# Two self-attention stages of a four-layer network: values projected inside the query/key loop, score banks claimed first, four banks for the projections

## The chip, the core and the metric

The kernel runs on one core of a Trainium2 chip, in one launch. The metric is the device time of one execution in microseconds. A profile is one further execution, recorded by the hardware. Engines are named as in the profile: PE is TensorE's matmul (PEld its weight load), DVE VectorE, ACT ScalarE, POOL GpSimd, SP the engine that issues most transfers.

## The reference, cut to what matters

Twelve stages run in a row on `x` (16 sequences of 64 tokens, width 256, float32): four layers of cross attention, self attention and feed-forward. Each reads a layer norm of `x` and adds its output to `x`, so no stage can begin before the one before it has finished the rows that it needs. Two of the twelve are touched:

```python
# layer 0 self attention (16 heads of 16), causal softmax
cq = gelu(x @ wq + bq);   ckv = gelu(x @ wkv + bkv)          # 256 -> 64
q = gelu(concat(cq @ wqc + bqc, rope(x @ wqr + bqr)))
k = gelu(concat(ckv @ wkc + bkc, rope(x @ wkr + bkr)))
v = ckv @ wv + bv
out = softmax(mask(q k^T / 4)) v @ wo + bo
# layer 1 self attention (16 heads of 16), causal linear attention
q, k, v = split(x @ w_qkv.T + b_qkv);   q, k = elu(q) + 1, elu(k) + 1
out = (cumsum(k v) q) / (cumsum(k) q + 1e-6) @ w_out.T + b_out
```

## The kernel before, in words

The 1024 tokens lie as 8 tiles of 128 rows, two sequences to a tile. Both stages have the same two parts.

**Projections.** `norm_T` (L347) turns the normalised rows into `xnT` (features on partitions, 1024 tokens along the row) with sixteen PE transposes and four copies. Then queries and keys are projected in halves of 512 tokens, one PSUM bank each.

- `L0_attn` (L1037) has four jobs `(d, h)`: d is 0 for queries and 1 for keys, h the half. `narrow` projects to 64 columns and ACT applies Gelu into `cl[d]`. `turned` projects the rotary part; ACT copies its two halves swapped into `sw`, and DVE makes `r`, `sw` and their sum (L1087, L1091). `wide`, one job later, projects `cl[d]` up to 128 columns, and `gelu` takes it and `r` through ACT: for queries straight into `qT`, for keys into `g`, from which DVE writes two masked copies into `k2` (L1102).
- `L1_attn` (L1233) has eight blocks: for each half h, c = 0, 1 (queries) and c = 2, 3 (keys). ACT makes `e` and `z` (L1262, L1263), DVE joins them (L1265), and for keys also writes two masked copies into `k2` (L1267).

After the last of these, `pair_values` (L1008) makes the values. POOL clears `V` and writes its two columns of ones (L1014, L1016; no order is imposed on these). Four times it then takes a bank, has PE project two token tiles into it, and has DVE add the bias in four instructions of 64 partitions (L1030).

**Attention.** A software pipeline over the 8 tiles. `scores(t)` writes 128 queries by 64 keys for all heads into half of `S4`, a tile of four banks; DVE masks it (L1142 `Sx` in layer 0, L1293 `A` in layer 1). In layer 0 a row maximum (L1149, DVE), its subtraction (L1150, POOL), an exponential (L1153, ACT) and transposes (`turn`) follow. `values(t)` multiplies by `V` and DVE divides (`pair_attend`, L1192), `back(t)` transposes, `out(t)` projects and `finish_x` adds to `x` and takes the next layer norm's statistics.

**What sets the order.** Between `self.fixed = True` and `False`, `mm`, `tr` and everything in `pinned` (L193) keep program order on their engine, so PE, ACT and DVE of these stages run as written. The allocator hands out PSUM banks; a matmul into a reused bank waits for the last reader of what was in it. The projections' pool `pst` has 6 banks (L1053, L1249). It is closed before the pool of `S4` is opened (L1123, L1275), so `S4` lies on banks that the projections and the values have used, and the first scores wait for the last bias addition of `V`.

Of the kernel before, what the change touches and what calls it, by code (L numbers as in the profile page):

```python
# [12 lines left out]
ALU = mybir.AluOpType  # L13
AX = mybir.AxisListType
PSUM = bass.MemoryType.PSUM

P = 128
B, S, D = 16, 64, 256
NT = B * S // P
# [157 lines left out]
class Net:  # L177
# [827 lines left out]
            "L0_attn_wv", "L0_attn_wo",  # L1005
        )

    def pair_values(self, pool, pp, xT, w, bias):  # L1008


        nc = self.nc
        n, k = w.shape[1], xT.shape[0]
        V = pool.tile([P, NT, 2, 8, 34], F32, tag="V", name="V")
        nc.gpsimd.memset(V, 0.0)  # L1014
        for i in range(2):
            nc.gpsimd.memset(V[i * S : (i + 1) * S, :, :, :, 32 + i], 1.0)  # L1016
        bias = bias.rearrange("p (a i f) -> p a i f", i=2, f=16)
        for t in range(0, NT, 2):
            ps = self.psum(pp, [P, 2, 8, 2, 16], "pst")
            for u in range(2):  # L1020
                for kc in range(n):
                    self.mm(
                        ps[:, u].rearrange("p a i f -> p (a i f)"),
                        xT[:, kc, (t + u) * P : (t + u + 1) * P], w[:k, kc, :],
                        kc == 0, kc == n - 1,
                    )
            for b in range(2):
                r = slice(b * S, (b + 1) * S)
                for i in range(2):
                    self.pinned(nc.vector.tensor_tensor(  # L1030
                        V[i * S : (i + 1) * S, t : t + 2, b, :, i * 16 : (i + 1) * 16],
                        ps[r, :, :, i, :], bias[r, :, i, :].unsqueeze(1).to_broadcast([S, 2, 8, 16]),
                        ALU.add,
                    ))
        return V

    def L0_attn(self, w):  # L1037


        nc, tc = self.nc, self.tc  # L1040
        wq, wkv, wqc, wkc, wqr, wkr, wv, wo = w
        with (
            tc.tile_pool(name="l0a", bufs=1) as wk,
            tc.tile_pool(name="l0am", bufs=4) as small,
        ):
            qT = wk.tile([P, 2, NTOK], F32, tag="qT", name="qT")

            k2 = wk.tile([P, 2, 2, NTOK], F32, tag="k2", name="k2")
            self.fixed = True
            with (  # L1050
                tc.tile_pool(name="l0an", bufs=1) as wn,
                tc.tile_pool(name="l0as", bufs=2) as sp,
                tc.tile_pool(name="l0a_t", bufs=6, space=PSUM) as pst,  # L1053
            ):
                xnT = self.norm_T(wn, pst, "pst")
                self.add_bias(1)
                jobs = [(d, h) for d in range(2) for h in range(2)]
                cl = [wn.tile([64, 1, NTOK], F32, tag=f"cl{d}", name="cl") for d in range(2)]
                names = (
                    (wq, "bq", wqc, "bqc", wqr, "bqr"), (wkv, "bkv", wkc, "bkc", wkr, "bkr"),  # L1060
                )
                par = self.c("par")
                rot = {}

                def narrow(d, h):
                    w1, b1 = names[d][:2]
                    tok = slice(h * 512, (h + 1) * 512)
                    ps = self.psum(pst, [P, 512], "pst")
                    self.project_T(ps[:64, :], w1, xnT, slice(None), tok)
                    self.pinned(nc.scalar.activation(  # L1070
                        cl[d][:, 0, tok], ps[:64, :], AF.Gelu, bias=self.pv(f"L0_attn_{b1}")[:64, :]
                    ))

                def turned(d, h):

                    wr, br = names[d][4:]
                    tok = slice(h * 512, (h + 1) * 512)
                    ps = self.psum(pst, [P, 8, S], "pst")
                    self.project_T(
                        ps.rearrange("p b s -> p (b s)"), wr, xnT, slice(None), tok  # L1080
                    )
                    sw = sp.tile([P, 8, S], F32, tag="sw", name="sw")
                    self.pinned(nc.scalar.copy(sw[0:64], ps[64:128]))
                    self.pinned(nc.scalar.copy(sw[64:128], ps[0:64]))
                    r = sp.tile([P, 8, S], F32, tag="r", name="r")
                    for o, i, b, c in ((r, ps, br, "cos0"), (sw, sw, br + "~", "sin0")):
                        self.pinned(nc.vector.scalar_tensor_tensor(  # L1087
                            o, i, self.pv(f"L0_attn_{b}"),
                            self.c(c).unsqueeze(1).to_broadcast([P, 8, S]), ALU.add, ALU.mult,
                        ))  # L1090
                    self.pinned(nc.vector.tensor_tensor(r, r, sw, ALU.add))  # L1091
                    rot[d, h] = r.rearrange("p b s -> p (b s)")

                def gelu(d, h, c, src, bias=0.0):
                    tok = slice(h * 512, (h + 1) * 512)
                    if d == 0:
                        self.pinned(nc.scalar.activation(qT[:, c, tok], src, AF.Gelu, bias=bias))
                        return
                    g = sp.tile([P, 512], F32, tag="g", name="g")
                    self.pinned(nc.scalar.activation(g, src, AF.Gelu, bias=bias))  # L1100
                    for i in range(2):
                        self.pinned(nc.vector.tensor_scalar(  # L1102
                            k2[:, c, i, tok], g, par[:, i : i + 1], None, ALU.mult
                        ))

                def wide(d, h):
                    w2, b2 = names[d][2:4]
                    tok = slice(h * 512, (h + 1) * 512)
                    ps = self.psum(pst, [P, 512], "pst")
                    self.mm(ps, w2[:64, 0, :], cl[d][:, 0, tok])  # L1110
                    gelu(d, h, 0, ps, self.pv(f"L0_attn_{b2}"))
                    gelu(d, h, 1, rot[d, h])

                for n in range(len(jobs) + 1):
                    if n < len(jobs):
                        narrow(*jobs[n])
                        turned(*jobs[n])
                    if n:
                        wide(*jobs[n - 1])
                V = self.pair_values(wk, pst, cl[1], wv, self.bv(0))  # L1120
            with (
                tc.tile_pool(name="l0at", bufs=2) as sp,
                tc.tile_pool(name="l0a_s", bufs=1, space=PSUM) as pss,  # L1123
                tc.tile_pool(name="l0a_p", bufs=2, space=PSUM) as pst,
                tc.tile_pool(name="l0a_a", bufs=1, space=PSUM) as psa,
            ):
                S4 = self.psum(pss, [P, 4, 2, 2, 2, S], "S4")
                state = {}

                def scores(t):  # L1130
                    ps = S4[:, :, t % 2]
                    for kc in range(2):
# [33 lines left out]
                def values(t):  # L1166
                    acc = self.psum(psa, [P, 8, 34], "acc")
                    state[t] = self.pair_attend(sp, acc, V, state[t], t, 0.0)

# [63 lines left out]
    def L1_attn(self, w):  # L1233
# [3 lines left out]
        nc, tc = self.nc, self.tc  # L1237
        wqkv, wout = w
        bqkv = self.pv("L1_attn_b_qkv")
        with tc.tile_pool(name="l1a", bufs=1) as wk:  # L1240
            qT = wk.tile([P, 2, NTOK], F32, tag="qT", name="qT")

            k2 = wk.tile([P, 2, B, 2, S], F32, tag="k2", name="k2")
# [1 line left out]
            with (  # L1245
                tc.tile_pool(name="l1an", bufs=1) as wn,
                tc.tile_pool(name="l1am", bufs=4) as small,
                tc.tile_pool(name="l1as", bufs=3) as sp,
                tc.tile_pool(name="l1a_t", bufs=6, space=PSUM) as pst,  # L1249
            ):  # L1250
                xnT = self.norm_T(wn, pst, "pst")
                self.add_bias(4)
                for h in range(2):
                    tok = slice(h * 512, (h + 1) * 512)
                    for c in range(4):
                        ps = self.psum(pst, [P, 512], "pst")
                        self.project_T(ps, wqkv, xnT, slice(c * P, (c + 1) * P), tok)

# [2 lines left out]
                        bias = bqkv[:, c : c + 1]  # L1261
# [4 lines left out]
                        for i in range(2 * (c // 2)):  # L1266
# [2 lines left out]
                                z.rearrange("p (b s) -> p b s", s=S),  # L1269
                                self.c("par")[:, i : i + 1], None, ALU.mult,  # L1270
                            ))
                V = self.pair_values(wk, pst, xnT, wqkv[:, :, 512:768], self.bv(3))
            with (
                tc.tile_pool(name="l1at", bufs=2) as sp,
                tc.tile_pool(name="l1a_s", bufs=1, space=PSUM) as pss,  # L1275
                tc.tile_pool(name="l1a_a", bufs=2, space=PSUM) as psa,
            ):
                S4 = self.psum(pss, [P, 4, 2, 2, 2, S], "S4")
                state = {}

                def scores(t):
                    ps = S4[:, :, t % 2]
                    for kc in range(2):
# [1079 lines left out]
```

## Time and profile before

| what | us |
|---|---|
| three runs | 3265.1, 3266.31, 3282.47 (median 3266.31) |
| the profiled execution | 3275.31 |
| its span, first to last instruction | 3273.5 |
| PE busy in the span | 3021.5 (92%) |
| DVE, ACT, POOL busy | 1261.0, 1362.1, 371.6 |
| mean granted TensorE clock | 0.953 |
| layer 0: first projection to last matmul of the values | 520.79 to 544.48 |
| layer 0: first scores, first mask `Sx` | 552.88, 554.13 |
| layer 1: first projection to last matmul of the values | 1707.16 to 1729.66 |
| layer 1: first scores, first mask `A` | 1732.72, 1733.90 |

All times inside the trace count from the span's start. In a row of the timeline the columns are: start, duration of the whole group, engine, source line, operation, output and inputs with sizes, number of instructions, and in brackets the idle time before it on its engine and what ended it. A float32 matmul of the program is two PE instructions in the trace. A busy PE is not PE at full clock: the clock that was granted is a column of its own. The share of busy time is an average over twelve stages; for a change inside two of them, what counts is the row that waits last there.

### The profile page before, as it was taken

To read this page: it belongs to the slowest core of one execution; us is meant where nothing else is said; L and a number is where in the kernel's file an instruction comes from. 1 tells how busy PE (TensorE), PEld (TensorE's weight loads), DVE (VectorE), ACT (ScalarE), POOL (GpSimd) and SP (SyncE) were. 2 spreads that over 40 slices of the span, in tenths; PEclk is the share of its full clock that TensorE was granted. 3 is DMA by queue.
4 is the path that set the end of the run, shared out by engine and by line. 5 is a ranking of instruction groups with operands and counts; after the bars stand their busy time and mean duration, and the time that the engine had idled before them with its cause. 6 is when DMAs were issued, how large, how long until landed. Compare 5 with 4: busy or idle time off the path is not lost. (4 is left out here: it accounts for less than half of the span.)

```text
span 3273.5 us, 67440 instructions
## 1 busy us (share of the span) xinstructions
PE 3021.5 (92%) x28567; PEld 2263.0 (69%) x28567; DVE 1261.0 (39%) x3415; ACT 1362.1 (42%) x2699; POOL 371.6 (11%) x538
## 2 busy tenths in 40 slices
PE   7999997699799999999998999999979798889798
PEld 5666664599556666666666777777748676778697
DVE  6888884422244444444446521221242100035200
ACT  5888884211233333333333522222222387763111
POOL 0000001233200000000010000000012311111232
PEclk9999998699899999999997999999988899999799
DMA  6334431389211121211257011111208555510497
GB/s 216 106 130 134 134 108 42 134 287 323 63 61 61 61 81 44 78 61 61 81 174 221 28 46 55 61 41 61 77 17 300 161 180 187 175 56 1 152 328 241
DMA packets 178362, 395.09 MB, mean 121 GB/s; under 512 B 11446, under 2 KB 142270, under 8 KB 165214
## 3 DMA queue, kind: packets, MB, share of 16 engines
q1 hardware_dynamic: 165070, 372.91, 33.0%
q0 software_dynamic: 11712, 16.00, 2.4%
q8 instruction: 225, 3.69, 0.5%
q10 hardware_dynamic: 1280, 1.88, 0.2%
q14 instruction: 75, 0.61, 0.1%
HBM read 375.02 MB, written 16.12 MB: 119 GB/s over the span
## 5 line engine op out<-in xcount | busy, mean ns | idle before, releaser
L199 PE MATMUL acc<-ctx,st 128*128 128x257 f32 (+1 forms) x1664 | 397.2, 383 | 0.0
L199 PE MATMUL pss<-qk,ctxT 128*128 128x512 f32 (+1 forms) x832 | 388.8, 592 | 0.6 <-DVE qk L634 0.6
L199 PEld LDWEIGHTS acc<-ctx,st 128*128 128x128 f32 (+1 forms) x1664 | 310.1, 190 | 94.6 <-issue 35.6
L459 DVE CUSTOM_DVE_ANT_0 Sx<-s,mneg 128x384 f32<-128x384 f32 (+1 forms) x512 | 264.2, 570 | 88.6 <-PE s L199 88.6
L650 DVE TENSOR_TENSOR top<-pss,top 128x512 f32<-128x512 f32 x192 | 132.7, 691 | 402.4 <-ACT st L645 402.3
L203 PE MATMUL pst<-cst,Sx 128*128 128x128 f32 (+1 forms) x1736 | 255.8, 286 | 25.5 <-ACT Sx L1369 10.3
L674 ACT ACTIVATE st<-st 128x512 f32<-128x512 f32 (+1 forms) x208 | 130.6, 629 | 292.5 <-DVE st L673 292.5
L935 ACT ACTIVATE Pr<-pss 128x512 f32<-128x512 f32 (+1 forms) x512 | 219.9, 523 | 62.1 <-PE pss L199 60.7
L503 ACT ACTIVATE PT<-pst 128x384 f32<-128x384 f32 x512 | 215.1, 489 | 63.4 <-PE pst L203 62.3
L203 PEld LDWEIGHTS pst<-cst,Sx 128*128 128x128 f32 (+1 forms) x1736 | 188.7, 143 | 73.1 <-ACT PT L503 27.8
L199 PEld LDWEIGHTS pss<-qk,ctxT 128*128 128x128 f32 (+1 forms) x832 | 154.1, 186 | 120.7 <-issue 102.7
L645 ACT COPY st<-pss 128x512 f32<-128x512 f32 (+1 forms) x208 | 121.8, 585 | 201.5 <-PE pss L199 201.5
L199 PE MATMUL pso<-W,hT 128*128 128x256 f32 x884 | 200.9, 379 | 0.0
L199 PE MATMUL pst<-wst,ctxT 128*128 128x256 f32 (+1 forms) x832 | 183.4, 380 | 0.0
L199 PE MATMUL psk<-ctxT,wst 128*128 128x512 f32 (+1 forms) x512 | 181.8, 513 | 0.8 <-ACT qT L797 0.8
L199 PEld LDWEIGHTS pso<-W,hT 128*128 128x128 f32 x884 | 163.2, 190 | 19.7
L199 PEld LDWEIGHTS pst<-wst,ctxT 128*128 128x128 f32 (+1 forms) x832 | 153.5, 186 | 25.9 <-issue 2.7
L199 PE MATMUL pss<-q,ctxT 32*128 32x128 f32 (+1 forms) x3328 | 149.6, 298 | 13.6 <-issue 9.5
L199 PEld LDWEIGHTS psk<-ctxT,wst 128*128 128x128 f32 x512 | 88.3, 190 | 93.7 <-issue 92.1
L356 POOL TENSOR_TENSOR x<-x,bvec 128x256 f32<-128x256 f32 x40 | 29.8, 746 | 1079.2 <-ACT xn L317 1079.2
L837 DVE TENSOR_TENSOR v<-pst,bvec 128x512 f32<-128x512 f32 (+1 forms) x112 | 73.1, 653 | 204.4 <-PE pst L199 204.4
L478 ACT ACTIVATE Sx<-Sx,neg 128x384 f32<-128x384 f32 (+1 forms) x256 | 145.8, 620 | 11.5 <-DVE neg L469 11.3
(394 smaller groups left out, 4479.5 us busy)
## 6 DMA issues: line engine op xcount, KB each, us to landing
ctxT<-in_ctxT_dram SPq DMA_DIRECT2D x64, 1601.0 KB
W<-in_L_experts_dram SPq DMA_DIRECT2D x61, 1024.0 KB
ctx<-in_ctx_dram SPq DMA_DIRECT2D x32, 1536.0 KB
W<-in_L_experts_dram SPq DMA_DIRECT2D x23, 1536.0 KB
ctx<-in_ctx_ones_dram SPq DMA_DIRECT2D x16, 1632.0 KB
ctx<-in_ctx_one_dram SPq DMA_DIRECT2D x16, 1542.0 KB
W<-in_L_experts_dram SPq DMA_DIRECT2D x23, 768.0 KB
W<-in_L_experts_dram SPq DMA_DIRECT2D x15, 1028.0 KB
```

The lines of the kernel that those rows point to most:

```text
L199: self.pinned(self.nc.tensor.matmul(out, lhsT, rhs, start=start, stop=stop))
L203: self.pinned(self.nc.tensor.transpose(out, in_, self.ident[:n, :n]))
L356: self.nc.gpsimd.tensor_tensor(self.x[:, t, :], self.x[:, t, :], self.bv(i), ALU.add)
L459: self.pinned(nc.vector.tensor_tensor_reduce(out=Sx[:, j, :n], in0=ps[j][:, :n], in1=st["mneg"][:, o : o + n], op0=ALU.add, op1=ALU.max, s ...
L478: self.pinned(nc.scalar.activation(Sj[j], Sj[j], AF.Identity, bias=st["neg"][:, j - 2 : j - 1]))
L503: self.pinned(nc.scalar.activation(PT, ps, AF.Exp))
L645: pin(nc.scalar.copy(st[:kn], ps[:kn]))
L650: pin(nc.vector.tensor_tensor(top[b][:kn], ps[:kn], top[b][:kn], ALU.max))
L674: pin(nc.scalar.activation(st, st, AF.Exp, scale=HD**-0.5))
L837: nc.vector.tensor_tensor(o, ps[:kn, :n, :], bv[:kn].to_broadcast([kn, n, D]), ALU.add)
L935: nc.scalar.activation(st["Pr"][:kn, g : g + n, j, :], ps[j][:kn, :n, :], AF.Silu)
```

## The change

`pair_values` is split. What is left of the name allocates `V` and has POOL clear it; the new `two_values(V, t, ...)` does one quarter of the rest: four (layer 0: two) matmuls into one bank, and four additions.

```diff
+    def two_values(self, V, t, pp, xT, w, bias):
...
+        ps = self.psum(pp, [P, 2, 8, 2, 16], "pst")
+        for u in range(2):
+            for kc in range(n):
+                self.mm(
...
+        for b in range(2):
...
+            for i in range(2):
+                self.pinned(self.nc.vector.tensor_tensor(
```

In layer 0 the keys' jobs come first, and two quarters of the values follow `wide` of each of the keys' two jobs. `S4` is opened at the top of the stage, with a pool of its own, and `pst` has 4 banks:

```diff
+            tc.tile_pool(name="l0a_s", bufs=1, space=PSUM) as pss,
         ):
+            S4 = self.psum(pss, [P, 4, 2, 2, 2, S], "S4")
...
-                tc.tile_pool(name="l0a_t", bufs=6, space=PSUM) as pst,
+                tc.tile_pool(name="l0a_t", bufs=4, space=PSUM) as pst,
...
-                jobs = [(d, h) for d in range(2) for h in range(2)]
+                jobs = [(d, h) for d in (1, 0) for h in range(2)]
...
+                V = self.pair_values(wk)
                 for n in range(len(jobs) + 1):
                     if n < len(jobs):
                         narrow(*jobs[n])
                         turned(*jobs[n])
                     if n:
                         wide(*jobs[n - 1])
-                V = self.pair_values(wk, pst, cl[1], wv, self.bv(0))
+                    if 1 <= n <= 2:
+                        for t in (4 * n - 4, 4 * n - 2):
+                            self.two_values(V, t, pst, cl[1], wv, self.bv(0))
```

In layer 1 `S4` and `pst` change in the same way, and a quarter of the values stands ahead of blocks 0 and 2 of each half:

```diff
+                V = self.pair_values(wk)
                 for h in range(2):
                     tok = slice(h * 512, (h + 1) * 512)
                     for c in range(4):
+                        if c % 2 == 0:
+                            self.two_values(
+                                V, 4 * h + c, pst, xnT, wqkv[:, :, 512:768], self.bv(3)
+                            )
                         ps = self.psum(pst, [P, 512], "pst")
...
-                V = self.pair_values(wk, pst, xnT, wqkv[:, :, 512:768], self.bv(3))
```

In the built program the number of instructions on each engine is the same, except for a few that only wait. The order of POOL's and SP's instructions does not change anywhere, and outside these two stages every instruction of every engine keeps its place and its waits.

More of the change, by code (lines that the diff above doesn't have):

```diff
@@ L1006, in load_L0_attn, with pair_values @@
         )
-    def pair_values(self, pool, pp, xT, w, bias):
+    def pair_values(self, pool):
         nc = self.nc
-        n, k = w.shape[1], xT.shape[0]
         V = pool.tile([P, NT, 2, 8, 34], F32, tag="V", name="V")
@@ L1016, in pair_values @@
             nc.gpsimd.memset(V[i * S : (i + 1) * S, :, :, :, 32 + i], 1.0)
+        return V
+    def two_values(self, V, t, pp, xT, w, bias):
+        n, k = w.shape[1], xT.shape[0]
         bias = bias.rearrange("p (a i f) -> p a i f", i=2, f=16)
[L1018 to L1035, printed above, removed]
+        ps = self.psum(pp, [P, 2, 8, 2, 16], "pst")
+        for u in range(2):
+            for kc in range(n):
+                self.mm(
+                    ps[:, u].rearrange("p a i f -> p (a i f)"),
+                    xT[:, kc, (t + u) * P : (t + u + 1) * P], w[:k, kc, :],
+                    kc == 0, kc == n - 1,
+                )
+        for b in range(2):
+            r = slice(b * S, (b + 1) * S)
+            for i in range(2):
+                self.pinned(self.nc.vector.tensor_tensor(
+                    V[i * S : (i + 1) * S, t : t + 2, b, :, i * 16 : (i + 1) * 16],
+                    ps[r, :, :, i, :], bias[r, :, i, :].unsqueeze(1).to_broadcast([S, 2, 8, 16]),
+                    ALU.add,
+                ))
     def L0_attn(self, w):
@@ L1119, in L0_attn @@
                         wide(*jobs[n - 1])
-                V = self.pair_values(wk, pst, cl[1], wv, self.bv(0))
+                    if 1 <= n <= 2:
+                        for t in (4 * n - 4, 4 * n - 2):
+                            self.two_values(V, t, pst, cl[1], wv, self.bv(0))
             with (
                 tc.tile_pool(name="l0at", bufs=2) as sp,
-                tc.tile_pool(name="l0a_s", bufs=1, space=PSUM) as pss,
                 tc.tile_pool(name="l0a_p", bufs=2, space=PSUM) as pst,
@@ L1126, in L0_attn @@
             ):
-                S4 = self.psum(pss, [P, 4, 2, 2, 2, S], "S4")
                 state = {}
@@ L1239, in L1_attn @@
         bqkv = self.pv("L1_attn_b_qkv")
-        with tc.tile_pool(name="l1a", bufs=1) as wk:
+        with (
+            tc.tile_pool(name="l1a", bufs=1) as wk,
+            tc.tile_pool(name="l1a_s", bufs=1, space=PSUM) as pss,
+        ):
+            S4 = self.psum(pss, [P, 4, 2, 2, 2, S], "S4")
             qT = wk.tile([P, 2, NTOK], F32, tag="qT", name="qT")
@@ L1248, in L1_attn @@
                 tc.tile_pool(name="l1as", bufs=3) as sp,
-                tc.tile_pool(name="l1a_t", bufs=6, space=PSUM) as pst,
+                tc.tile_pool(name="l1a_t", bufs=4, space=PSUM) as pst,
             ):
@@ L1255, in L1_attn @@
                     for c in range(4):
+                        if c % 2 == 0:
+                            self.two_values(
+                                V, 4 * h + c, pst, xnT, wqkv[:, :, 512:768], self.bv(3)
+                            )
                         ps = self.psum(pst, [P, 512], "pst")
@@ L1271, in L1_attn @@
                             ))
-                V = self.pair_values(wk, pst, xnT, wqkv[:, :, 512:768], self.bv(3))
             with (
                 tc.tile_pool(name="l1at", bufs=2) as sp,
-                tc.tile_pool(name="l1a_s", bufs=1, space=PSUM) as pss,
                 tc.tile_pool(name="l1a_a", bufs=2, space=PSUM) as psa,
             ):
-                S4 = self.psum(pss, [P, 4, 2, 2, 2, S], "S4")
                 state = {}
```

## The prediction

> **What bounds the kernel now.** I read the page first. PE is busy 92% of the span, so only stages in which PE stands still can give much; the chain that ended last is scattered over a dozen lines and names neither stage. So I asked the view of waits for the two stretches that the change touches (waiting engine and line, releaser, total us, times, longest).
>
> ```profile
> DVE r L1087 <- ACT sw L1084: 12.4, 4, 5.3
> ...
> PE S L199 <- DVE V L1030: 8.4, 1, 8.4
> ```
>
> ```profile
> PE S L199 <- DVE V L1030: 3.1, 1, 3.1
> DVE wa L1760 <- DMA wst<-in_L_w2T_dram: 2.2, 1, 2.2
> ```
>
> In both stages the first scores wait for the last bias addition of the values, 8.4 and 3.1 us. All of that is not yet a gain: the scores also need keys, queries and then DVE. So I read the timeline of layer 0 there.
>
> ```profile
> 530.71 0.75 DVE L1087 SCALAR_TENSOR_TENSOR r<-pst,pvec,cst 128x512 f32<-128x512 f32 x1 [1.64 <-ACT sw L1084]
> ...
> 532.15 0.69 DVE L1091 TENSOR_TENSOR r<-r,sw 128x512 f32<-128x512 f32 x1
> ...
> 540.87 3.61 PE L199 MATMUL pst<-wst,cl 64*128 64x256 f32 x16
> ...
> 542.48 3.39 DVE L1102 TENSOR_SCALAR k<-g,cst 128x512 f32<-128x512 f32 x8
> ...
> 545.78 6.96 DVE L1030 TENSOR_TENSOR V<-pst,bvec 64x256 f32<-64x256 f32 x16
> ...
> 552.88 1.16 PE L199 MATMUL S<-k,qT 32*64 32x128 f32 x32 [8.39 <-DVE V L1030]
> 554.13 1.23 DVE L1142 TENSOR_TENSOR Sx<-S,cst 128x1024 f32<-128x1024 f32 x1 [1.40 <-PE S L199]
> ```
>
> PE has the values' matmuls done at 544.48, while DVE is behind: after the last rotary sum it has eight masked copies (3.39) and sixteen additions (6.96) left, in a row. DVE is the late engine. Ahead of that it had gaps: each rotary group waits for ACT's `sw` copies, 12.4 us in four waits. Layer 1:
>
> ```profile
> 1707.16 15.60 PE L199 MATMUL pst<-xnT,wst 128*128 128x512 f32 x32
> ...
> 1722.59 7.07 PE L199 MATMUL pst<-wst,xnT 128*128 128x256 f32 x32
> ...
> 1722.79 0.69 ACT L1262 ACTIVATE e<-pst,pvec 128x512 f32<-128x512 f32 x1 [0.45 <-PE pst L199]
> ...
> 1724.82 0.88 DVE L1267 TENSOR_SCALAR k<-z,cst 128x512 f32<-128x512 f32 x2
> 1725.62 6.96 DVE L1030 TENSOR_TENSOR V<-pst,bvec 64x256 f32<-64x256 f32 x16
> ...
> 1732.72 1.12 PE L199 MATMUL S<-qT,k 32*128 32x64 f32 x32 [3.06 <-DVE V L1030]
> 1733.90 1.23 DVE L1293 TENSOR_TENSOR A<-S,cst 128x1024 f32<-128x1024 f32 x1 [1.32 <-PE S L199]
> ```
>
> Here PE works to 1729.66 without a gap, and DVE's additions end 3 us later.
>
> Last, the table by stretches (stretch, its length, busy us of PE, PEld, DVE, ACT and POOL, granted clock, DMA share, GB/s):
>
> ```profile
> 531.00:545.00 14.00, 13.49 (x38) 5.98 (x36) 8.41 (x16) 8.44 (x15) 0.00 (x0) 1.00 0.01 2
> 545.00:553.00 8.00, 0.12 (x8) 0.15 (x16) 7.53 (x19) 1.17 (x1) 0.00 (x0) 0.62 0.00 0
> 553.00:570.00 17.00, 11.12 (x208) 8.66 (x208) 10.46 (x10) 6.25 (x8) 7.61 (x4) 0.50 0.01 1
> 1711.00:1730.00 19.00, 18.66 (x60) 11.02 (x58) 14.20 (x28) 9.72 (x16) 0.00 (x0) 1.00 1.09 335
> 1730.00:1735.00 5.00, 1.12 (x32) 1.01 (x32) 3.61 (x7) 0.00 (x0) 0.00 (x0) 0.97 1.06 333
> 1735.00:1747.00 12.00, 11.82 (x166) 10.66 (x167) 5.50 (x10) 0.37 (x1) 0.00 (x0) 0.50 1.10 340
> ```
>
> Projections run at clock 1.00; after the first gap layer 0's pipeline runs at 0.50, and layer 1's soon after its own.
>
> **The change, layer 0.** No arithmetic is added: eight matmuls and sixteen additions of values move forward, and the keys' jobs change places with the queries'. The order of the built program gives DVE's list from the second rotary group on: rotary group, four copies into `k2`, two quarters of values; the same again; the last rotary group; then the first mask. Durations from the rows: a rotary group 530.71 to 532.84, 2.13 us; four copies 3.39/2 = 1.70; two quarters 6.96/2 = 3.48. From 530.71, where the second group starts in both kernels: 532.84, 534.54, 538.02 (values), 540.15, 541.85, 545.33 (values), 547.46. That is 16.75 us without a gap, if its inputs come in time. For that I walk PE: a `narrow`/`turned` pair takes 3.84 (row at 530.45), a `wide` 1.0, a quarter 0.90 (3.61/4). `wide` 0 ends at 530.4, two quarters at 532.2, the third pair at 536.0, `wide` 1 at 537.0, two quarters by 538.9, the fourth pair by 542.8, `wide` 2 at 543.8 and `wide` 3 at 544.7. ACT's copies for the third rotary group are then done by 537.4, DVE wants them at 538.0; for the fourth by 544.1, wanted at 545.3. So DVE is never kept waiting.
>
> The new wait: the first mask in the built program waits for ACT's last Gelu, of the fourth rotary group (0.62 and two hand-offs of about 0.05): 547.46 + 0.7 = 548.2. Behind it on DVE stands the whole attention pipeline. The scores themselves wait only for ACT's Gelu of the first half of queries, near 545.5, and take 1.25, ready by 546.8. So the first mask moves from 554.13 to 548.2, **5.9 us**. The 8.4 us wait is not the gain, because DVE still has its additions to make and is late again; what is won is its waiting for `sw` and nothing else.
>
> **Layer 1.** The order on DVE is a quarter of values, joins of two query blocks, a quarter, joins and four copies of two key blocks, and again. PE's sum is as before, so it ends near 1729.7; but its last matmuls are now those of a key block, not of values. Behind a key block's matmuls come two ACT steps, a join and two copies: in the old trace the last block's matmuls end at 1722.6 and its copies at 1725.7, 3.1 us. So DVE is free at 1732.8 and the first `A` begins there instead of at 1733.90: **1.1 us**. The 3.1 us wait of PE is exchanged for a tail of the same length on ACT and DVE. DVE's wait for the weights at 1709.78 plus the 2.29 reduction behind it now stands ahead of the first quarter's additions: done at 1713.8. The first key block takes their bank, and PE comes to it only at about 1715.8, so 2 us cover that; a load later by more than 2 us would be paid in full.
>
> **Four banks.** Reusing a bank earlier adds waits on PE, in front of everything queued there. Layer 0: the third quarter waits for the first one's additions (536.3, wanted 537.0), the fourth for ACT's Gelu of `wide` 1 (about 538.0, wanted 537.9), the fourth pair for the second quarter (538.0, wanted 538.9), `wide` 3 for the third quarter (543.6, wanted 543.8). Cost 0.1 to 0.3, hidden by DVE's list, which ends later. Layer 1: each block finds its bank free by 1.5 us or more. The first transposes of layer 1 now wait for the previous stage's last addition to `x`, ending at 1701.33, 0.8 us later than they started; the rest of them wait until 1706.5 for the last normalised rows anyway, so it costs nothing; without that cover, 0.8. POOL's clearing of `V` (3.73) keeps its place in POOL's queue in both stages, ahead of the statistics of the last tile; SP's queue is unchanged. The program behind the stages is unchanged too, and each stage starts from `x`, so a shift carries to the end. The next stage's weights are fetched only after routing, and from 519 to 615 the DMA share is 0.03 or less, so no transfer sets an end there that stays while the start moves.
>
> **Sum.** 5.9 + 1.1 = 7.0. Against the profiled execution: 3275.31 - 7.0 = 3268.3. That execution lies 9.0 above the median of the three runs; carried to the median, 3266.31 - 7.0 = **3259**.
>
> **A rule that speaks against it.** The Trainium skill, "TensorE: Matmul & The Clock Gate", section "A second HAM failure mode: psum-queue depth-cycling", tells of a kernel that cycled through its PSUM banks so that TensorE stood idle briefly between groups, and its clock swung between half and full. Fewer banks are a step that way. The row: with six banks the stretch 531 to 545 has PE busy 13.49 of 14.00 at clock 1.00. By my walk four banks add 0.3 us of gaps, so I stay with the row, 3259. By the rule the projections would drop to 0.50: layer 0's 14.3 us of matmul work from 530.4 on ends at 559.0 and the first mask, 2.1 us of rotary group and 0.7 later, comes near 561, +7; layer 1's 18.7 us from 1711 on end at 1748.4 and with the tail of 3.1 at 1751.5, +17.6. Together 3291.
>
> **Rivals.** *The clock holds in the pipelines* (0.14). The gap of PE ahead of layer 0's second scores shrinks from 8.4 to about 3 us, and layer 1's start changes. If the pipelines then ran at full clock: four transposes take 1.11 or 0.66 in the two clocks, so five tiles save 2.3; a turn of layer 1 has scores 1.99 or 1.12, values 1.93 or 1.13, projection 2.08 with transposes or 1.13 + 0.38, so four turns save up to 8. 3249. Against it: 553 to 570 has PE busy 11.1 of 17 and stays at 0.50, and the gaps between scores remain.
>
> *Nothing is won* (0.11): DVE's sixteen additions, now made while PE writes other banks, take longer. The gain of layer 0 is gone if the list of 16.75 takes 22.6, a third more. For it: nothing in the trace shows this mix. Against it: the first additions at 545.78 and the last have nearly one duration, 409 to 430 ns. 3266. That the change doesn't reach its aim (scores still waiting for the values) is excluded by the built order: their waits name ACT alone in layer 0 and nothing new in layer 1.
>
> *Slower* (0.09): the clock falls in the projections, as reckoned above, 3291. Half clock for t us costs t/2, so it decides from about 14 us at 0.50 in the two projections together.
>
> **Numbers.** The likeliest case, 0.66, has its own range 3253 to 3264 (the first masks within 1 us, the pipelines within 2 of their old length each). The three runs before scatter by 17 us, and a difference under 0.5% (16 us) is about what a measurement of this kernel can't tell from none. Faster by more: most of the clock's case and some scatter, 0.12. Slower by more: 0.09. Within: 0.79. The range, 3247 to 3270, takes in the clock's case in its upper part and the case of no gain; it leaves out the slower one.
>
> **What would show it.** Layer 0: the first mask near 548.2 (counted from an equal start), DVE without a gap from 530.7 to 547.5, PE's wait for `V` gone. Layer 1: PE without a gap to 1729.7, the first `A` near 1732.8 with the last copy of `k2` before it. Clock 1.00 in both projections. I am wrong if a projection shows 0.50, if PE waits for DVE by more than 1 us inside one, or if the pipelines of eight tiles change in length.

## The result, and the profile after

| | before | after |
|---|---|---|
| first series, median | 3277.48 us (3265.1 to 3287.73, 20 runs) | 3266.31 us (3258.15 to 3279.37, 20 runs) |
| ratio, 95% interval | | 0.9970 [0.9960, 0.9980] |
| second series, median | 3276.39 us (30 runs) | 3269.95 us (22 runs) |
| ratio, 95% interval | | 0.9982 [0.9972, 0.9993] |
| profiled execution, its span | 3275.31, 3273.5 us | 3270.24, 3268.5 us |
| mean granted clock in the span | 0.953 | 0.952 |

The change makes the kernel faster by 0.2 to 0.3%, which lies within the 0.5% that were called no difference. The three runs shown before the prediction lay low: over 106 runs of three later series the kernel before has a median of 3276.85 us, not 3266.31. (That the first series after has the same 3266.31 is chance.)

The profiled execution after, in the same views. Waits first, layer 0's stretch and then layer 1's (waiting engine and line, releaser, total us, times, longest):

```profile
DVE r L1091 <- ACT sw L1088: 8.2, 2, 6.6
...
PE S L199 <- DVE Sx L1148: 4.6, 2, 3.2
```

```profile
PE S L199 <- DVE A L1305: 3.3, 1, 3.3
```

PE's waits for `V`, 8.4 and 3.1 us, are gone. Each is replaced by one of 3.2 or 3.3 us between the scores of the first and of the second tile. DVE's waits for `sw` fell from 12.4 us in four to 8.2 in two, the ones ahead of the values. The timeline of layer 0:

```profile
532.09 0.75 DVE L1091 SCALAR_TENSOR_TENSOR r<-pst,pvec,cst 128x512 f32<-128x512 f32 x1 [1.64 <-ACT sw L1088]
...
535.73 3.49 DVE L1033 TENSOR_TENSOR V<-pst,bvec 64x256 f32<-64x256 f32 x8
...
538.29 2.26 PE L199 MATMUL pst<-wst,cl 64*128 64x256 f32 x8
...
542.88 3.49 DVE L1033 TENSOR_TENSOR V<-pst,bvec 64x256 f32<-64x256 f32 x8
...
548.55 0.63 ACT L1101 ACTIVATE qT<-r 128x512 f32<-128x512 f32 x1 [1.21 <-DVE r L1095]
549.21 1.22 DVE L1148 TENSOR_TENSOR Sx<-S,cst 128x1024 f32<-128x1024 f32 x1 [0.69 <-ACT qT L1101]
```

After the wait ahead of 532.09 no DVE row up to the last rotary sum (547.83, 0.69 long) has a bracket: the list is contiguous. ACT's last Gelu follows, and the mask waits for that alone. The ring of four banks shows in one row: the second pair of values takes 2.26 us where the first took 1.89. Layer 1's last block:

```profile
1725.25 3.60 PE L199 MATMUL pst<-xnT,wst 128*128 128x512 f32 x8
...
1728.78 1.12 PE L199 MATMUL S<-qT,k 32*128 32x64 f32 x32
...
1730.91 0.88 DVE L1282 TENSOR_SCALAR k<-z,cst 128x512 f32<-128x512 f32 x2
1731.90 1.23 DVE L1305 TENSOR_TENSOR A<-S,cst 128x1024 f32<-128x1024 f32 x1
```

The scores now start at once, but DVE has the last copies of `k2` to make, as the prediction had it: 3.1 us from the last projection to `A`. The table by stretches (columns as before; the clock is the third number from the end):

```profile
531.00:545.00 14.00, 13.89 (x38) 6.04 (x38) 12.63 (x27) 6.60 (x12) 0.00 (x0) 1.00 0.01 2
...
553.00:570.00 17.00, 11.78 (x182) 9.30 (x182) 9.82 (x11) 6.25 (x8) 8.29 (x5) 0.60 0.01 2
1711.00:1729.00 18.00, 18.00 (x62) 10.10 (x61) 11.98 (x25) 8.96 (x15) 0.00 (x0) 1.00 1.10 336
...
1734.00:1746.00 12.00, 12.00 (x168) 10.38 (x164) 6.23 (x11) 0.74 (x2) 0.00 (x0) 0.50 1.10 337
```

Both projections keep clock 1.00 and both pipelines still run mostly at half clock.

**How executions are compared.** PE starts each stage at half clock, and the moment at which it comes up differs from execution to execution: in layer 0 the first rotary group on DVE stands 5.9 to 7.5 us behind the first projection. The first mask of layer 0 is therefore counted from that group (the expectations below count from the first projection, so they are larger by this much); counted so, all kernels with the same layer-0 code agree within 0.02 us. In layer 1 it is counted from the first projection, and the old code there gives 26.74 and 26.96, the new one 25.52 to 25.88. A pipeline runs from the start of the first mask to the start of the last addition to `x`. The mean clock of the kernel before is that of one series; in the two others it is 0.9516.

| kernel | mask L0 | mask L1 | pipe L0 | pipe L1 | mean clock of its runs | ratio [95%] |
|---|---|---|---|---|---|---|
| before | 27.20 | 26.74 | 62.05 | 46.33 | 0.9513 | 1 |
| after | 20.90 | 25.88 | 61.94 | 41.40 | 0.9525 | 0.9970 [0.9960, 0.9980] |
| after, again | 20.90 | 25.52 | 61.24 | 46.93 | 0.9519 | 0.9982 [0.9972, 0.9993] |
| layer 0 only | 20.90 | 26.96 | 60.98 | 46.34 | 0.9519 | 0.9981 [0.9971, 0.9991] |
| layer 1 only | 27.20 | 25.55 | 59.84 | 44.15 | 0.9509 | 0.9989 [0.9977, 1.0000] |
| values only | 20.90 | 25.85 | 60.63 | 44.13 | 0.9521 | 0.9976 [0.9965, 0.9988] |
| banks only | 25.83 | 25.70 | 60.09 | 41.40 | 0.9531 | 0.9973 [0.9962, 0.9983] |
| key copies on GpSimd | 19.77 | 25.52 | 60.58 | 46.93 | 0.9530 | 0.9972 [0.9962, 0.9982] |
| keys first | 20.90 | 24.51 | 61.40 | 40.87 | 0.9532 | 0.9967 [0.9955, 0.9980] |
| filler | 20.92 | 25.69 | 59.99 | 36.69 | 0.9552 | 0.9957 [0.9944, 0.9970] |
| two banks | 33.10 | 29.35 | 60.72 | 46.92 | 0.9503 | 1.0032 [1.0018, 1.0046] |
| before with filler | 27.20 | 26.96 | 63.69 | 39.76 | 0.9543 | 0.9994 [0.9982, 1.0007] |
| copies, keys first, filler | 19.77 | 24.81 | 59.91 | 38.03 | 0.9578 | 0.9954 [0.9940, 0.9968] |
| early scores | 19.78 | none | 61.05 | none | 0.9548 | 0.9980 [0.9968, 0.9992] |

The first mask moved by 6.30 us in layer 0 (forecast 5.9) and by 0.9 and 1.2 us in layer 1 (forecast 1.1). Layer 1's pipeline is 4.9 us shorter in one execution of the changed kernel and 0.6 us longer in another. The new code of layer 1 shows 41.40, 44.15 and twice 46.93 us ("after", "layer 1 only", "after, again", "key copies"), the old one twice 46.3: the length belongs to the execution, and whether the new code meets the short one more often is not settled.

**The clock's share.** Within one program the runs scatter about a line: each 0.001 of mean granted clock goes with 2.0 us (95%: 1.8 to 2.3; 42 runs of the changed kernel and 106 of the one before, one slope for both). The means of these runs differ by 8.3 us (95%: 6.2 to 10.4). At equal clock the difference is 6.9 us (5.7 to 8.0); the other 1.5 go with a mean clock higher by 0.0007, whose own interval, 0.0008 either way, includes none. Taken apart, the changed kernel's first series (beside 47 runs of the kernel before) gives 7.6 us at equal clock and its second (beside its own 30) 5.5, so the 6.9 is less sharp than its interval. And a mean clock is itself moved by what a kernel does: this is a comparison, not a cause.

### The profile page after: what moved, and what is told of

Same layout as the page of the kernel before. It is cut to its first block, busy times and chain, and to the rows that moved or that the text cites. A ratio compares the mean times of both kernels' runs of the same rounds, so it can differ in the third digit from the quotient of the medians.

```text
span 3268.5 us, 67442 instructions
## 1 busy us (share of the span) xinstructions
PE 3028.5 (93%) x28567; PEld 2267.5 (69%) x28567; DVE 1261.3 (39%) x3415; ACT 1361.5 (42%) x2699; POOL 370.9 (11%) x538
## 5 line engine op out<-in xcount | busy, mean ns | idle before, releaser
L199 PEld LDWEIGHTS pss<-q,ctxT 32*128 32x128 f32 (+1 forms) x3328 | 120.0, 193 | 47.8 <-issue 36.9
```

What stands on the lines that cost most here:

```text
L199: self.pinned(self.nc.tensor.matmul(out, lhsT, rhs, start=start, stop=stop))
```

## The experiments

**The two layers apart.** One layer as in the changed kernel, the other as before.

> Layer 0 changed, layer 1 as before (the values in a row after the projections, six banks). My theory (the gain is VectorE's list in layer 0 without its gaps): from layer 0's first projection matmul to its first mask 28.3 us as in the changed kernel (33.3 before), layer 1's 26.7 as before, time 5 us below before, ratio 0.9985. Rival (layer 1's pipeline at a better clock is part of the gain): its pipeline, first mask to last addition to x, is 46 as before here, and the missing 4 to 5 us show against the changed kernel. Rival (scatter of other stages makes the 0.3%): ratio 0.997 here too, with layer 1 unchanged.

> Layer 1 changed, layer 0 as before. My theory: layer 1's first mask comes 25.9 us after its first projection matmul (26.7 before), layer 0's after 33.3, and the time falls by 1 us only, ratio 0.9997. Rival (the clock of layer 1's pipeline): its pipeline takes 41 instead of 46, the time falls by 5 to 6, ratio 0.998.

Layer 0 alone moves the mask by 6.30 us, layer 1 alone by 1.2; the ratios 0.9981 and 0.9989 are 6.2 and 3.6 us, their sum 9.8 beside the 9.8 and 5.9 of the two series of the whole change. So no effect of one stage on the other is seen, but the two intervals are 3 to 4 us wide either way and would hide one of that size. My ratios, 0.9985 and 0.9997, lie in the intervals, and layer 0 is the larger part, as expected.

**The two ideas apart.** Once the values moved forward, with six banks and `S4` opened where it was; once `S4` claimed first and four banks, with the values and the jobs in their old order:

```diff
-                jobs = [(d, h) for d in (1, 0) for h in range(2)]
+                jobs = [(d, h) for d in range(2) for h in range(2)]
...
-                    if 1 <= n <= 2:
-                        for t in (4 * n - 4, 4 * n - 2):
-                            self.two_values(V, t, pst, cl[1], wv, self.bv(0))
+                for t in range(0, NT, 2):
+                    self.two_values(V, t, pst, cl[1], wv, self.bv(0))
```

> Both stages with the values inside the projections and the keys first, but with six banks and the tile of the scores opened after the projections, as before. My theory: VectorE's list is what counts, so layer 0's first mask after 28.3 to 29, layer 1's after 26 to 26.3, time as the changed kernel within 1 us. Rival (it is the banks that carry the gain): layer 0's first mask after 31 or more.

> Both stages with the score tile opened outside and four banks, but the values in a row after the projections and the queries' jobs first, as before. TensorE no longer waits for the values, but the masks stand behind the sixteen additions on VectorE. My theory: layer 0's first mask after 31.9 (1.4 earlier than before), layer 1's after 25.4 to 25.6 (1.2 earlier), time 2.6 us below before, ratio 0.9992. Rival (the wait of 8.4 and 3.1 us for the values is what was lost): layer 0's after 25 to 27, ratio 0.997.

In layer 0 the moved values give the whole 6.30 us, and the banks alone 1.37: the scores no longer wait, but DVE's sixteen additions still stand ahead of the mask. In layer 1 either idea alone gives 0.9 to 1.0 us, and both together no more than 0.9 to 1.2: they remove the same step, the mask's wait of 1.3 us for the scores behind the last addition. The total of "banks only" missed my 0.9992 and is what the rival named (0.997), though the mask stands where I had it. 8.8 us faster by its ratio, it is not explained by its masks (2.4 us); its mean clock, 0.0018 above the kernel before's, is worth 3.6 by the slope above, and the rest is inside its interval. The totals therefore don't tell the two ideas apart; only the masks do.

**The changed kernel again**, in one series with the next three.

> The changed kernel once more, beside its variants. First theory (a sum of local terms of 7 us, plus what the clock adds): at equal mean granted clock 7 to 8 us below the kernel before, and the first mask of layer 0 again near +28.3 us and that of layer 1 near +25.9 us from the first projection of its stage. Its mean clock over all runs tells whether the clock's share is systematic: 0.0010 or more above the kernel before's again if it is (then the ratio is 0.9965 to 0.997), the same within 0.0004 if it was chance (then the ratio is 0.9977).

The masks came where they were. In this series the kernel before has a mean clock of 0.9516, so the surplus is 0.0003: the case of chance, whose ratio was expected at 0.9977 and is 0.9982. At equal clock this series alone gives 5.5 us (3.7 to 7.3), less than the 7 to 8 that I had expected, which the interval just reaches. Layer 1's pipeline took 46.93 us.

**Is DVE's list the bound in layer 0?** The eight copies go to GpSimd:

```diff
-                        self.pinned(nc.vector.tensor_scalar(
+                        self.pinned(nc.gpsimd.tensor_scalar(
                             k2[:, c, i, tok], g,
```

> Layer 0's eight masked copies of the keys are issued by GpSimd instead of VectorE. If VectorE's contiguous list bounds layer 0's projections (the step of the prediction), 3.4 us leave that list and the first mask comes at +25.0 to +26.2 instead of +28.3 us, when TensorE's own list or ScalarE's last Gelu has become the bound: 2 to 3 us below the changed kernel, ratio to the kernel before 0.996 to 0.9965. If ScalarE's last Gelu or TensorE was the bound all along, the mask stays within 0.5 us of +28.3. [...]

Yes, but with little behind it: 3.4 us leave DVE's list and the mask gains 1.13, not 2 to 3. DVE then waits for PE and ACT. In the following rows of that kernel PE has no bracket up to its last projection, so PE is the bound that was 1.1 us away:

```profile
539.32 1.06 DVE L1095 TENSOR_TENSOR r<-r,sw 128x512 f32<-128x512 f32 x1
...
543.07 1.98 PE L199 MATMUL pst<-cl,wst 64*128 64x512 f32 x4
543.17 0.58 ACT L1087 COPY sw<-pst 64x512 f32<-64x512 f32 x1 [1.23 <-PE pst L199]
...
544.38 0.75 DVE L1091 SCALAR_TENSOR_TENSOR r<-pst,pvec,cst 128x512 f32<-128x512 f32 x1 [0.58 <-ACT sw L1088]
```

A copy costs 1.56 us on GpSimd (median of eight; the longest 2.08) against 0.42 on DVE, all of it beside other work. The additions on DVE, which read PSUM, kept their 3.48 for eight. But the two rotary sums that ran beside GpSimd's copies, `r<-r,sw`, took 1.06 us instead of 0.69; the two that did not kept 0.69. Both kernels built on this one show the same, so moving work to GpSimd isn't free for DVE; here PE as the bound hid it.

**Is the tail what counts in layer 1?** Key blocks first, then query blocks, values last in each half:

```diff
-                    for c in range(4):
-                        if c % 2 == 0:
-                            self.two_values(
-                                V, 4 * h + c, pst, xnT, wqkv[:, :, 512:768], self.bv(3)
-                            )
+                    for c in (2, 3, 0, 1):
...
+                        if c % 2:
+                            self.two_values(
+                                V, 4 * h + 2 * (c < 2), pst, xnT, wqkv[:, :, 512:768], self.bv(3)
+                            )
```

> In layer 1 the key blocks are projected ahead of the query blocks in each half, and the values after them. The tail behind the last matmul then is four additions of values (1.4 us and an access) instead of the key block's bias on ScalarE and two copies on VectorE (3.1 us). Tail theory: the first mask at +24.5 to +25.0 instead of +25.9 us, about 1.2 us less, ratio 0.9965 to 0.997. If the order of work does not matter to the tail: +25.9. The layer-1 pipeline behind it takes 41.4, 44 or 46 us by the number of turns that TensorE runs at half clock, and that is not set by this edit.

As expected: the mask at +24.51, 1.0 us earlier than in the changed kernel of the same series. (The four additions of the tail took 1.73 us, not 1.4.)

**Is it PE's pause that drops the clock?** Extra work whose result nothing reads, in both stages behind `scores(0)` (`wout` in layer 1):

```diff
+                    if n == 0:
+                        fill = self.psum(psa, [P, D], "py")
+                        for _ in range(6):
+                            self.mm(fill, wo[:, 0, :P], wo[:, 0, :])
```

> Six dense 128x256 matmuls, whose result nothing reads, are added in both stages between the scores of the first and of the second tile, where TensorE waits 3.2 us for VectorE: about 2.8 us of extra TensorE work. Clock theory (the pipelines are paced by half-clock turns that begin with TensorE's pause at the first masks): the pipeline of layer 1 takes 41.4 us or less and that of layer 0 under 61.9, and the mean granted clock rises by 0.0005 or more. Rival (the clock in the pipelines does not answer to that pause): both pipelines unchanged or up to 1 us longer each, the clock within 0.0004 of the changed kernel, ratio to the kernel before 0.997 to 0.998.

More work, less time: 0.9957, where the changed kernel of that series has 0.9982. Layer 1, that changed kernel and then the filler, four us to a row, from the row with the first mask on:

```profile
1726.18:1730.18 4.00, 1.20 (x31) 1.20 (x32) 2.61 (x4) 0.00 (x0) 0.00 (x0) 0.91 1.05 334
1730.18:1734.18 4.00, 4.00 (x72) 3.81 (x70) 2.08 (x4) 0.00 (x0) 0.00 (x0) 0.50 1.10 341
1734.18:1738.18 4.00, 4.00 (x66) 3.48 (x63) 2.08 (x4) 0.37 (x1) 0.00 (x0) 0.50 1.10 343
```

```profile
1725.62:1729.62 4.00, 3.89 (x44) 3.17 (x44) 2.77 (x4) 0.00 (x0) 0.00 (x0) 1.00 1.10 345
1729.62:1733.62 4.00, 3.71 (x106) 3.30 (x102) 3.21 (x5) 0.37 (x1) 0.00 (x0) 1.00 1.10 340
1733.62:1737.62 4.00, 4.00 (x86) 3.56 (x88) 3.12 (x10) 0.37 (x1) 0.00 (x0) 1.00 1.10 340
```

In the second and third rows PE is busy 3.71 to 4.00 of 4.00 in both kernels, but with the filler at full clock, with 106 and 86 matmul records in a row instead of 72 and 66. Layer 1's pipeline takes 36.69 us, 10 less than in the changed kernel of that series. In layer 0 the gain is 1.25 us; PE soon stands still there again (busy 2.81 of 5.00 us from 555 on).

**Does the filler need the change?** The same six matmuls in the kernel before.

> The kernel before, unchanged but for the six unused 128x256 matmuls in both stages between the scores of the first and of the second tile (extra work). If the filler's gain is a matter of TensorE's pause and the clock alone, it comes here too: layer 1's pipeline takes 36 to 38 us instead of 46.3, and the ratio is 0.997 or less by that alone, with the masks where they were (+33.3 and +26.7 us). In layer 0 the pause of 8.4 us ahead of the first scores stands before the filler and is not covered, so its pipeline stays at 60 to 62 us. If the filler needs the changed order, layer 1's pipeline stays at 46 and the ratio is 1.000.

Wrong in the total, and only near in the part. In layer 1 PE has already paused 3.06 us ahead of the first scores, so the filler runs mostly at half clock and delays the second scores, before it brings the clock up for the rest: 39.76 us, 6.6 less than before, not 8 to 10.

```profile
1740.17 4.54 PE L199 MATMUL py<-wst 128*128 128x256 f32 x12
```

In the changed kernel with filler the same group takes 2.86 us. In layer 0, behind the pause of 8.4 us, it takes 5.07 and makes the pipeline 1.6 us longer. The four terms of the table thus give 4.7 us less (157.6 against 162.3), the ratio 0.9994 (2 us, and its interval reaches 5.9). The change, by taking the wait for `V` away, is what makes the filler cheap.

**Is it the pause or the narrow matmuls?** The next two kernels: first all that helped (key copies on GpSimd, keys first, filler in both stages). Then layer 0 as in that one, and in layer 1 no filler, but the scores and masks of tiles 0 and 1 inside the last projections:

```diff
+                        if h and c > 1:
+                            scores(c - 2)
...
-                    if n < NT:
+                    if 2 <= n < NT:
                         scores(n)
```

> The changed kernel with all that helped: layer 0's key copies on GpSimd, layer 1's keys first, and the filler in both stages. If the terms add: masks at +27 and +24.5 us, pipelines 60 and 36.7 us, so about 2.3 us below the filler alone and ratio 0.995 to 0.996. If the clock answers to more than the pause: the pipeline of layer 1 goes back to 41 to 47 us and the ratio to 0.997.

> Layer 0 as in the version with all that helped; layer 1 without the filler, and instead the scores and masks of tiles 0 and 1 are made inside the last projections (keys first, values last), so that TensorE need not pause for the first mask. If the pause is what drops the clock: layer 1's pipeline runs at 0.9 or above in its first 12 us, from the last projection to the last addition to x it takes 36 us or less, and the ratio is 0.995 or less, the lowest of all. If the clock falls because of what the pipeline's matmuls are (narrow ones), it falls here as well: 40 us or more and ratio 0.996 to 0.997.

The first has the lowest ratio of all, 0.9954 (15 us), and beats both kernels; but it is not told apart from the filler alone by these intervals. In the second, the windows from the end of the projections on, and the scores of tile 5:

```profile
1724.14:1726.33 2.19, 0.00 (x1) 0.03 (x1) 1.99 (x5) 0.00 (x0) 0.00 (x0) 1.00 1.09 347
1726.33:1736.50 10.17, 10.17 (x224) 8.95 (x225) 6.07 (x17) 3.02 (x4) 1.01 (x3) 1.00 1.10 334
```

```profile
1740.09 1.98 PE L199 MATMUL S<-qT,k 32*128 32x64 f32 x32 [2.92 <-DVE A L1273]
```

The narrow matmuls run at 1.00 without any filler, so they alone don't make the clock fall. A pause of 2.19 us is survived; one of 2.92, behind DVE's passes over the next stage's weights, is followed by scores at half clock (1.98 instead of 1.12); the last section shows where the two pauses lie. From the last projection to the last addition to `x` this execution takes 36.2 us, where I had expected 36 or less, and the stage 62.6 from its first projection, as with the filler (62.4), against 72.5 in the changed kernel's second profile. But its ratio is 0.9980, not 0.995: the profiled execution was one of its quickest (3260.7 us, the runs go to 3277.05). Where the other runs lose their time wasn't profiled and stays open.

**The price of the ring**, and the rule cited against the change: two banks instead of four (`bufs=4` to `bufs=2` in both stages).

> The changed kernel with two banks for the projections instead of four, so that almost every group of matmuls waits for the group two before it to be read out. My theory (a bank's price is the wait for its reader, and the clock stays up while the gaps are short): the first mask of layer 0 comes 2 to 6 us later than the changed kernel's +28 us and that of layer 1 0 to 2 us later than +25.7, with the granted clock of both projections at 0.95 or above; ratio to the kernel before 0.998 to 1.000. Rival (the rule about cycling through banks): the clock in the projections shows 0.50 in part, and the masks come over 7 us later in layer 0 and over 5 us later in layer 1.

The rival was right for layer 0, where the mask comes 12.2 us later:

```profile
534.20 3.48 DVE L1033 TENSOR_TENSOR V<-pst,bvec 64x256 f32<-64x256 f32 x8
536.07 5.98 PE L199 MATMUL pst<-xnT,wst 128*64 128x512 f32 x8 [2.78 <-DVE V L1033]
```

The third job's matmuls wait 2.78 us for a bank that DVE's additions still read; then they run at half clock, 5.98 us where four banks take 3.85, and the fourth job the same way in 6.41. The two slower pairs make PE's list 4.7 us longer; its waits for banks in this stretch add to 8.6 us, the longest two of 2.78. Together that is 13.3, and 12.2 reach the mask, which fits the 1.1 us that PE's list had to spare. In layer 1 the waits were 0.2 to 1.4 us and the clock stayed at 1.00, as I had it, but the mask came 3.7 us later, more than my 2. The ratios (1.0032 against 0.9982 and 0.9970) make it 16 to 20 us in all.

## Why the prediction was right, point by point

- **The base.** 3275.31 - 7.0 was carried to a median of three runs that lay 10 us low. The prediction of 3259 is therefore 7 us under the first series' median (3266.31) and 10 under the middle of both series (3268.9). The measured time lies in the stated range of 3247 to 3270, but outside the 3253 to 3264 given for the likeliest case, and 3266 is the very figure of the rival "nothing is won": on that base the total could not tell the two apart, and that it lay in the range owes something to luck. What tells them apart is the kernel before beside it (3277.48) and the masks. The difference of 7.0 is what held: 6.9 (5.7 to 8.0) at equal clock, 8.3 without that. Set against the profiled execution, as it was before it was carried over, it gives 3268.3.
- **DVE is late in layer 0; its list of 16.75 us without a gap sets the first mask.** Right. Measured: 532.09 to 548.52, 16.43 us, then ACT and the mask at +0.69. From the first rotary group the mask moved by 6.30 us, not 5.9: the list was 0.3 shorter than the sum of rounded rows. That the waiting for `sw` "and nothing else" is won was too strong: it gives 5.4 us; another 0.7 comes from the mask, which waited 1.40 us for the scores before and now waits 0.69 for the Gelu. The copies to GpSimd show that PE's own list ends 1.1 us before DVE's, so the bound was named rightly, with little room under it.
- **Layer 1 exchanges a tail for one of the same length.** Right: 1.1 forecast, 0.9 and 1.2 measured, and "keys first", which shortens the tail, moves the mask by another 1.0. What the working didn't say is that the claimed banks alone give this too.
- **Four banks cost 0.1 to 0.3 us, hidden.** Right: one group of 2.26 instead of 1.89, so 0.37 and a little over the forecast, PE busy 13.89 of 14.00, clock 1.00. The ring isn't free below that: two banks cost 12.2 and 3.7 us.
- **The rule on cycling through banks.** With four banks the row was the better guide, as argued. With two, layer 0's clock fell, as the rule tells. The clock record has half clock from 533.70 on, 0.4 us into the first pause of 2.78, after 3.42 us in which PE was busy for only 2.08; so it answers to the pauses together and not to that one. The sum by the rule had +7 for layer 0 (its own terms give 561.8, so +7.7) and +17.6 for layer 1; with two banks they lost 12.2 and 3.7, and layer 1's clock stayed at 1.00. It was of the right kind for layer 0, at the wrong number of banks, and wrong for layer 1 at both.
- **The rival that the clock holds in the pipelines.** It didn't come: 0.60 and 0.50 in the rows. Its price for layer 1, "up to 8", was short of its own rows: the three differences of a turn make 2.2 us, so four make 9; and the 2.08 us are the projection alone, the transposes beside it took 0.63, so a turn would save 2.9 and four 11.5. The filler made the case come in layer 1 and won 10.
- **"I am wrong if the pipelines of eight tiles change in length".** This test was badly chosen. Layer 1's pipeline took 41.4 to 46.9 us in executions of the same code, so 4.9 us of one profile speak neither for nor against a step. By the sign as it was written the prediction would have failed. I took the one length that the profile showed as fixed; it varies with the clock.

## What to carry to other kernels

When an engine waits for another at the end of a stage, add up that other engine's list before counting the wait as a gain: of 8.4 + 3.1 us of waiting 7 were won, because DVE, not PE, was late. Count an effect of a few us from the nearest common event in both traces, and look at the granted clock of many runs before believing one profile. And before a stretch of narrow matmuls, a pause of PE of 3 us can cost more than the pause: filling it was worth as much again as the change itself.

## What the runs showed of the hardware

**When the clock falls.** In the clock records of the 14 traces every stretch at one clock is a whole number of steps of 3.41 us. What PE did within one step counts, more than the length of a pause. Of 126 steps at full clock in which the profile has PE busy for less than 40%, all were followed by half clock; of 417 with 40 to 65%, 184; of 9493 with more, 33. The two pauses of "early scores", by these steps:

```profile
1721.99:1725.41 3.42, 2.15 (x9) 1.35 (x8) 2.31 (x5) 1.28 (x3) 0.00 (x0) 1.00 1.10 343
1725.41:1728.82 3.41, 2.49 (x66) 2.23 (x66) 1.86 (x6) 0.00 (x0) 0.00 (x0) 1.00 1.10 332
1735.65:1739.06 3.41, 1.52 (x36) 1.16 (x34) 2.67 (x3) 1.42 (x3) 0.00 (x0) 1.00 1.09 330
```

The pause of 2.19 us lies across the end of a step and leaves PE busy 63 and 73% of the two; the clock stays. The one of 2.92 us (from 1737.17) puts 1.89 us into one step, which leaves 45%; half clock follows from 1739.06 on. So length alone is no bound: in layer 0's pipeline of the changed kernel a pause of 1.56 us (at 595.23) was followed by half clock, and in its second profile one of 2.89 us (at 584.69) was not.

**When it comes back.** The way back goes with the kind of work. After the pause of 2.92 us it took about 6 us. In layer 1 of the changed kernel's second profile PE was busy 3.89 to 4.00 of every 4 us and stayed at 0.50 from 1730.18 to 1766.18, 36 us. The Trainium skill, "TensorE: Matmul & The Clock Gate", section "What's actually happening", has the clock return after one busy window of about 3.4 us; these rows show a PE that the profile counts as busy almost without a break for ten times as long, and no return, so the measurement decides. The six 128x256 matmuls brought it back within their own 4.5 us. Over all 14 traces, of the steps at half clock with PE busy for 95% or more, full clock followed after 21 of 21 that were mostly 128x512 matmuls and after 98 of 105 that were mostly 128x256, but after 2 of 73 that were mostly `32*128 32x64` and `128*64 128x34`, the forms of layer 1's scores and of the values. In 31 such narrow steps that began at full clock it held. Which property of these matmuls counts was not tried.
